# Marks, moved copies and banks at both ends of a two-block transformer kernel, and rotary tables spread by transfers

## The chip, the cores and the metric

The kernel runs on one core of a Trainium2 chip. The core has TensorE (PE, the matrix unit), VectorE (DVE), ScalarE (ACT) and GpSimd (POOL), which run their own instruction queues and wait for each other by semaphores, and SyncE (SP), whose queue issues all transfers of this kernel to the 16 DMA engines. The metric is the device time of one execution in microseconds.

## The reference

Two transformer blocks work one after the other on x of 32 sequences, 64 tokens each, 512 features, all in float32. The first block has 8 query heads and one head of keys and values, rotary positions that come from an input, and a gated MLP of width 2048; the second has 16 query heads in four groups, keys and values from a latent of 128, and no MLP. Both norms are scaled by a condition per sequence.

```python
def block0(x, pos_ids, t, ...):
    h = ada_rms(x, t, ln1_w, ln1_tw)          # x * rsqrt(mean(x*x)) * w * (1 + t @ tw.T)
    q, k, v = h @ Wq.T, h @ Wk.T, h @ Wv.T    # 8 heads, 1 head, 1 head of 64
    q, k = rope(q, pos_ids), rope(k, pos_ids) # x * cos(pos * freq) + rotated(x) * sin(pos * freq)
    x = x + softmax(q @ k.T / 8) @ v @ Wo.T
    h = ada_rms(x, t, ln2_w, ln2_tw)
    return x + silu(h @ Wg.T) * (h @ Wu.T) @ Wd.T

def block1(x, t, ...):
    scale, shift = split(t @ W_ada.T + b_ada)
    h = layernorm(x) * (1 + scale) + shift
    q, c = h @ Wq.T, h @ Wkd.T
    k, v = c @ Wku.T, c @ Wvu.T               # 4 groups of 32
    return x + softmax(rope(q) @ rope(k).T / sqrt(32)) @ v @ Wo.T
```

## The kernel before

**Tiling.** The 2048 tokens are cut into eight units of 256 tokens (four sequences). Features lie on the 128 partitions, so x of a unit is a tile of 128 x 4 x 256. Each unit passes through `attention0`, `mlp` and `attention1`. The MLP goes in eight steps of hidden blocks; each matrix product there is done with seven block products instead of eight, from sums of weight blocks (`combine` makes four sums per set of weights on VectorE or GpSimd during unit 0, `done_with` stores them to DRAM, and later units load them back). A set is a tile of 7 x 256 columns; five buffers with the tag `mw` hold sets, and `load_sets` issues the load of a set when a buffer comes free.

**Order of work.** The pieces of work are generators. Between the ends, `Order.run` picks the next piece by costs and latencies that the generators yield, so that attention of neighbouring units fills in between the MLP steps of the current one. A scheduler below that places each engine's instructions by their priority and its own timing, unless an order is forced. At both ends the order is written by hand: the string `FIRST` for the start and `LAST` for the end, one letter per piece: `a` and `b` are two units (0 and 1 at the start, 6 and 7 at the end), `m` a piece of the modulations, `i` a pair of idle matmuls (in `LAST`). TensorE is held to that order by `ordered`; the other engines are not.

**The start.** SP loads positions, constants, the first modulation weights, x and the attention weights. `first_angles` makes sine and cosine of position times frequency for units 0 and 1, a quarter of the partitions per sequence. `modulation` multiplies the condition with its weights, copies the product to SBUF (`rows`, L313), turns it on TensorE (`pt_mod`) and makes the scale s0a (later s0b, s1, t1). `rms` squares x on ScalarE and scales x by s0a, half on VectorE and half on GpSimd for the lean first two units (L518). `angles` makes the angles of two further units at a time; it is called at the end of `attention0` of units 1, 3 and 5, and its instructions may be placed earlier.

**Rotary tables.** The angles lie with 32 frequencies times 4 sequences on the partitions; the rotation of queries needs them with features on the partitions and sequences along the columns. `spread_out` (L409) does that with four matmuls by a matrix of zeros and ones, for sine and cosine together. `tables` calls it for units 2 to 7 and multiplies the PSUM result by the row of inverse roots into `cs` (L418, L419); units 0 and 1 use `tables_by_quarters`.

**PSUM.** Eight banks: two with the tag `at` for attention, two `gu`, four `acc`. In the middle attention uses `at` alone; at both ends `abank` goes around over all of them. `output` adds the output projection to x: at the end (`fine`) it works in four chunks of 128 features, two chunks in one bank (`po`, L535), each followed by an add on VectorE (L583) and a transfer out (L584). `context` of `attention1` copies its PSUM result to SBUF in two copies per bank on ScalarE (L911).

Of the kernel before, what the change touches and what calls it, by code (L numbers as in the profile page):

```python
# [1 line left out]

# [1 line left out]

# [6 lines left out]
F32 = mybir.dt.float32  # L11
# [6 lines left out]
P = 128  # L18
# [27 lines left out]
ROUND = 12582912.0  # L46
WARM = 11
STAY = 14103
FIRST = "aaaaaaa bb a mm aa bb a bbb aa b mm a bb aa a m b a b m b a b".replace(" ", "")
EARLY = 4  # L50

LAST = "aa b aa b iii b aa ii b bb bbb aa aa bb aa aaaa bbbb bb bbbb".replace(" ", "")
TWO_PI = float(np.nextafter(np.float32(2 * np.pi), np.float32(0)))


# [43 lines left out]
@contextmanager  # L99
def ordered(tc, engine):  # L100

    traced = tc.nc.cur_bb.bb.instructions
    start = len(traced)
    yield
    mine = [i for i in traced[start:] if i.engine == engine]
    info = mybir.DependencyInfo(mybir.DependencyClass.NoSync, mybir.DependencyReason.DATA)
    for one, other in zip(mine, mine[1:]):
        tc.add_manual_dep(other, one.name, info, reason="order")


@with_exitstack
def two_blocks(ctx: ExitStack, tc: tile.TileContext, a: dict, out: bass.AP):
# [69 lines left out]
    def load_positions(u0):  # L182
        t = work("pos", [P, 2 * S], f"pos_{u0}", 1).bitcast(I32)
        nc.sync.dma_start(t, a["pos"][:, u0 * S : (u0 + 2) * S])
        positions.append(t)

    load_positions(0)
    small = fixed([P, C_ALL])
    nc.sync.dma_start(small, a["small"])
# [56 lines left out]
    def load_sets(upto):  # L246
        for n in range(len(sets), min(upto, len(sequence))):
# [8 lines left out]
                nc.sync.dma_start(t[:, 0:4], kept[i])  # L256
            sets[n] = t

    def combine(n):

        if n < len(sequence) and sequence[n][1] < NP:
            t, a21 = sets[n], odd[n]
            e = nc.gpsimd if n < 2 else nc.vector
            e.tensor_tensor(t[:, 0], a21, t[:, 6], ALU.add)  # L264
            e.tensor_tensor(t[:, 1], t[:, 0], t[:, 4], ALU.subtract)
            e.tensor_tensor(t[:, 2], t[:, 4], a21, ALU.subtract)
            nc.gpsimd.tensor_tensor(t[:, 3], t[:, 5], t[:, 1], ALU.subtract)
# [26 lines left out]
    load_x(1)  # L294
    load_mod(1)
    nc.sync.dma_start(wo0, a["wo0"])


    def modulation(i):

        dst = (s0a, s0b, s1, t1)[i]
        ps = abank(f"ps_mod{i}")
        for k in range(KC):
            for c in range(KC):
                nc.tensor.matmul(
                    ps[c * B : (c + 1) * B, :P],
                    condT[:, k, :],
                    mods[i][c, k],
                    start=(k == 0),
                    stop=(k == KC - 1),  # L310
                )
        rows = work("latT1", [P, UT], f"rows_{i}", 1)[:, :P]
        nc.vector.tensor_copy(rows, ps[:, :P])  # L313
        yield 1.2, 0.5
        pt = abank(f"pt_mod{i}")
        nc.tensor.transpose(pt[:, :P], rows, ident)
        got = pt[:, :P].rearrange("p (c b) -> p c b", b=B)
        v = vecs[:, KC * i : KC * (i + 1)].unsqueeze(2).to_broadcast([P, KC, B])
        if i < 2:
            nc.vector.scalar_tensor_tensor(dst, got, 1.0, v, ALU.add, ALU.mult)  # L320
        elif i == 2:
            nc.vector.scalar_tensor_tensor(dst, got, 1.0, v, ALU.add, ALU.add)
        else:
            nc.vector.tensor_tensor(dst, got, v, ALU.add)
        yield 0.1, 0.0
# [3 lines left out]
    def angles(u0):  # L329
# [38 lines left out]
        nc.scalar.activation(acc, hi, AF.Sin, scale=TWO_PI)  # L368
        nc.scalar.activation(rnd, prod, AF.Sin, scale=TWO_PI)
        nc.vector.tensor_tensor(rnd, rnd, sign, ALU.mult)  # L370
        if u0 + 2 < NU:
            load_positions(u0 + 2)

# [32 lines left out]
    def spread_out(ps, of):  # L406

        for b in range(US):
            nc.tensor.matmul(ps[..., b, :], spread[:, b], of, start=True, stop=True)  # L409

    def tables(u, r):

        ps = abank(f"tab_{u}").rearrange("p (i b s) -> p i b s", i=2, s=S)
        spread_out(ps, angle[:, :, u * S : (u + 1) * S])
        cs = work("cs", [P, 2, UT], f"cs_{u}", 1)
        cos, sin = cs[:, 0], cs[:, 1]
        ps = ps.rearrange("p i b s -> p i (b s)")
        nc.vector.tensor_tensor(cos, ps[:, 0], r, ALU.mult)  # L418
        nc.vector.scalar_tensor_tensor(sin, ps[:, 1], sign_of, r, ALU.mult, ALU.mult)  # L419
        return cos, sin  # L420

    def tables_by_quarters(u, few, room):
# [82 lines left out]
    def rms(u, s, h, room, name):  # L505

        x = x_units[u]
        lean = "lean" in room
        sq = tile4(room, "h", f"sq_{name}") if lean else work("sq", [P, KC, UT], f"sq_{name}", 1)
        nc.scalar.activation(sq, x, AF.Square)  # L510
        if lean:
            parts = [sq[:, k] for k in range(KC)]
            c = KC // 2
            for e, part in ((nc.vector, slice(0, c)), (nc.gpsimd, slice(c, KC))):
                to = h[:, part].rearrange("p c (b s) -> p c b s", s=S)
                of = x[:, part].rearrange("p c (b s) -> p c b s", s=S)
                by = s[:, part, US * u : US * (u + 1)].unsqueeze(3).to_broadcast([P, c, US, S])
                e.tensor_tensor(to, of, by, ALU.mult)  # L518
# [55 lines left out]
    def output(u, cT, w, name, last=False, fine=False):  # L574

        x = x_units[u]
        for h in range(2):
            po = abank(f"po_{name}_{h}").rearrange("p (c t) -> p c t", c=2)
            for c in range(2):
                o = 2 * h + c  # L580
                project(po[:, c], w, slice(o * P, (o + 1) * P), cT)
                if fine:
                    nc.vector.tensor_tensor(x[:, o], x[:, o], po[:, c], ALU.add)  # L583
# [12 lines left out]
    def attention0(u, room, early=None, late=None):  # L596
# [28 lines left out]
        if lean:  # L625
            few = space(room, "few", 3 * S, f"quarters_{u}").rearrange("p (k c) -> p k c", c=S)
            root_by_quarters(r, eps0, few[:, 0], f"ms_a{u}")
            kv = keys_values()
            yield 1.7, 0.0
            turn = query(0)  # L630
# [3 lines left out]
            cos, sin, r = tables_by_quarters(u, few, room)  # L634
        else:
            cos, sin = tables(u, r)
        yield 1.0, 0.0

        qT = tile4(room, "qT", f"qT0_{u}")
        turn = turn or query(0)  # L640
# [117 lines left out]
    def attention1(u, room):  # L758
# [139 lines left out]
        def context(t, pTs):  # L898
# [9 lines left out]
                    )  # L908
            to = cT[:, :, t * P : (t + 1) * P].rearrange("p c (b s) -> p b c s", s=S)
            for b in range(2):  # L910
                nc.scalar.copy(to[:, b], cx[:, b])  # L911

        ps = []
        for t in range(2):
# [159 lines left out]
    load_mod(3)  # L1074

    first = work("p0", [P, 1024], "p0_0", 1)
    ahead = Job(attention0(1, {"ring": "1", "lean": True}, late=lambda: angles(2)), A0)
    streams = {
        "a": attention0(0, {"ring": "0", "lean": True, "p": [first[:, :512], first[:, 512:]]}, early),
        "b": ahead.pieces,  # L1080
# [1 line left out]
    }  # L1082
    with ordered(tc, mybir.EngineType.PE):
        for name in FIRST:
            next(streams[name], None)
# [168 lines left out]
```

## Time and profile before

| | |
|---|---|
| median of 3 runs | 1048.79 us (1048.55 to 1049.76) |
| profiled execution, its own time | 1047.82 us |
| its span, first to last instruction | 1046.0 us |
| TensorE clock granted, mean | 0.992 |
| busy: PE, DVE, ACT, POOL | 1007.5, 548.7, 334.1, 436.4 us |
| DMA | 198.53 MB, mean 190 GB/s |

Busy times are the union of an engine's instructions; a float32 matmul is recorded as two. The waits name the engine whose event came last before an instruction could start. In a timeline each row has the start, the time from first start to last end, the engine, the source line, the operation, output and inputs with their sizes and the count; in brackets the idle time of that engine just before, with what ended it. The page's slices cut the span in 40 equal parts of 26 us; the digits are tenths.

### The profile page before, as it was taken

How to read it: one execution, taken by the hardware profiler on the slowest of the kernel's cores; microseconds unless marked ns; L12 is line 12 of the kernel's file. 1: busy time of each engine (PE TensorE's matmuls, PEld its weight loads, DVE VectorE, ACT ScalarE, POOL GpSimd, SP SyncE). 2: the span in 40 equal slices, each digit the busy share in tenths (PEclk: the TensorE clock that was granted, in tenths of full speed). 3: DMA queues.
4: the chain of work that ended last, by engine and by line, in shares of the span. 5: the costliest groups of instructions: out<-in, count | busy, mean ns of one | idle time of the engine just before them, and what ended most of it. 6: DMA issues, size and time to landing. Idle time of an engine off the chain costs nothing.

```text
span 1046.0 us, 21558 instructions
## 1 busy us (share of the span) xinstructions
PE 1007.5 (96%) x8578; PEld 936.4 (90%) x8578; DVE 548.7 (52%) x1379; ACT 334.1 (32%) x683; POOL 436.4 (42%) x521
## 2 busy tenths in 40 slices
PE   7899999999999998999999999999999999999987
PEld 6679989998999998999999989899999899999875
DVE  4966656454355376444664366652465425543372
ACT  5333112244123242143340342242323512333141
POOL 3424545544244532445342354324553334642351
PEclk8989999999999999999999999999999999999999
DMA  8816886553655563673646646446745547565201
GB/s 279 314 60 202 275 299 244 195 175 144 230 198 185 171 213 125 233 247 104 229 163 231 233 141 212 160 155 219 259 165 193 180 167 250 185 235 202 79 1 40
DMA packets 68850, 198.53 MB, mean 190 GB/s; under 512 B 7312, under 2 KB 16272, under 8 KB 68368
## 3 DMA queue, kind: packets, MB, share of 16 engines
q1 hardware_dynamic: 68752, 197.17, 54.5%
q8 instruction: 68, 1.11, 0.4%
q14 instruction: 30, 0.25, 0.1%
HBM read 180.37 MB, written 16.78 MB: 188 GB/s over the span
## 4 chain that ended last, share of the span: by engine, by line
PE 81%; DVE 8%; POOL 4%; DMA 4%; issue 2%; ACT 1%; SPq 0%; ACTq 0%; DVEq 0%; POOLq 0%
PE gu L937 33%; PE down L996 16%; PE q L535 10%; PE po L535 10%; DMA set<-in_wmlp 3%; PE sc L875 2%; PE pp L570 1%; PE cx L902 1%; PE lat L535 1%; PE sc L689 1%; PE kv L535 1%; PE cx L710 1%; DVE set L264 1%; DVE sm L563 1%; DMA x<-in_x 1%
## 5 line engine op out<-in xcount | busy, mean ns | idle before, releaser
L937 PE MATMUL gu<-h,set 128*128 128x128 f32 x2048 | 288.6, 277 | 6.8 <-DVE c L956 6.3
L937 PEld LDWEIGHTS gu<-h,set 128*128 128x128 f32 x2048 | 259.4, 193 | 16.2 <-issue 11.3
L937 PE MATMUL gu<-hc,set 128*128 128x128 f32 x1536 | 215.7, 276 | 0.0
L937 PEld LDWEIGHTS gu<-hc,set 128*128 128x128 f32 x1536 | 193.9, 193 | 1.0 <-issue 0.6
L975 POOL TENSOR_TENSOR act<-c,c 128x384 f32<-128x384 f32 x64 | 66.4, 1037 | 212.1 <-DVE c L963 138.2
L996 PE MATMUL down<-td,set 128*128 128x128 f32 x1024 | 137.7, 276 | 3.7 <-POOL td L978 2.5
L996 PEld LDWEIGHTS down<-td,set 128*128 128x128 f32 x1024 | 125.5, 192 | 5.7 <-POOL td L978 3.5
L949 ACT COPY e<-gu 128x128 f32<-128x128 f32 x128 | 33.7, 264 | 260.9 <-PE gu L937 244.9
L535 PE MATMUL po<-cT,stays 128*128 128x256 f32 x480 | 109.4, 382 | 3.4 <-DVE x L583 1.8
L535 PE MATMUL q<-h,stays 128*128 128x256 f32 x480 | 109.4, 381 | 0.0
L996 PE MATMUL down<-act,set 128*128 128x128 f32 x768 | 109.4, 278 | 0.0
L963 DVE TENSOR_TENSOR c<-gu,u 128x256 f32<-128x256 f32 x128 | 53.4, 419 | 106.5 <-PE gu L937 106.2
L951 DVE TENSOR_TENSOR u<-e,gu 128x128 f32<-128x128 f32 x128 | 36.1, 282 | 129.7 <-ACT e L949 129.1
L535 PEld LDWEIGHTS po<-cT,stays 128*128 128x128 f32 x480 | 89.7, 192 | 15.9 <-DVE x L583 2.6
L996 PEld LDWEIGHTS down<-act,set 128*128 128x128 f32 x768 | 97.7, 192 | 5.3 <-issue 3.2
L535 PEld LDWEIGHTS q<-h,stays 128*128 128x128 f32 x480 | 90.1, 191 | 12.3 <-issue 0.4
L565 POOL TENSOR_TENSOR p<-p,sm 128x512 f32<-128x512 f32 x40 | 41.6, 1058 | 121.5 <-DVE sm L564 115.6
L546 POOL TENSOR_TENSOR qT<-u_q,v_q 128x512 f32<-128x512 f32 x30 | 38.1, 1270 | 89.0 <-DVE v_q L545 88.9
L1032 ACT ACT_TABLE_LOAD x35 | 44.9, 1283 | 55.6 <-DVE c L963 55.1
L589 DVE TENSOR_TENSOR x<-x,po 128x512 f32<-128x512 f32 x28 | 19.2, 687 | 72.9 <-PE po L535 72.9
L977 POOL TENSOR_TENSOR td<-act 128x256 f32<-128x256 f32 x64 | 46.7, 730 | 5.6 <-DVE act L974 0.9
L1032 ACT ACTIVATE c<-gu 128x128 f32<-128x128 f32 x64 | 17.7, 277 | 85.6 <-DVE c L963 77.7
(264 smaller groups left out, 1336.6 us busy)
## 6 DMA issues: line engine op xcount, KB each, us to landing
set<-sums SPq DMA_DIRECT2D x168, 512.0 KB, 5.7
set<-in_wmlp SPq DMA_DIRECT2D x192, 384.0 KB, 4.7
sums<-set SPq DMA_DIRECT2D x24, 512.0 KB, 4.8
x<-in_x SPq DMA_DIRECT2D x8, 512.0 KB, 5.6
mod<-in_mod SPq DMA_DIRECT2D x7, 512.0 KB, 5.4
a<-in_wmlp SPq DMA_DIRECT2D x24, 128.0 KB, 3.1
out_x<-x SPq DMA_DIRECT2D x12, 256.0 KB, 2.6
stays<-in_wo SPq DMA_DIRECT2D x2, 1024.0 KB, 8.0
```

Source lines behind the costliest of these rows:

```text
L535: nc.tensor.matmul(ps, w[:, k, cols], h[:, k, :], start=(k == 0), stop=(k == KC - 1))
L546: nc.gpsimd.tensor_tensor(dst, u, v, ALU.add)
L565: nc.gpsimd.tensor_tensor(p8, p8, sm.unsqueeze(2).to_broadcast(wide), ALU.mult)
L875: nc.tensor.matmul(sc[b * S : (b + 1) * S, j * P : (j + 1) * P], qT[of, j, cols], kb[of, 2 * t + b].rearrange("p g k -> p (g k)"), start=True,
L937: nc.tensor.matmul(ps, w[:, slot, k * P : (k + 1) * P], b[of][:, k], start=start and k == 0, stop=k == 1, skip_group_check=True)
L949: nc.scalar.copy(e, ps[:, 0])
L951: nc.vector.tensor_tensor(u2, e, ps[:, 1], ALU.add)
L963: nc.vector.tensor_tensor(c.rearrange("p (a b) t -> p a b t", b=2)[:, :, 1], ps[:, 2:4], u2.unsqueeze(1).to_broadcast([P, 2, HT]), ALU.add,)
L975: nc.gpsimd.tensor_tensor(act[:, 1:4], gate[:, 1:4], c[:, 1:4], ALU.mult)
L977: nc.gpsimd.tensor_tensor(td[:, 0:2], act[:, 1:3], act[:, 0:2], ALU.subtract)
L996: nc.tensor.matmul(sums_of[u][p][:, c], w[:, slot, c * P : (c + 1) * P], b[of], start=q % NP == 0 and i % 2 == 0 and c == 0, stop=q % NP = ...
L1032: nc.scalar.activation(gate[2][:, 0], gate[0][:, 0], AF.Silu)
```

## The change

1. *First loads.* The first loads on SP are held to the written order, from positions to the output weights: positions, constants, modulation weights, x of unit 0, both attention weights, x of unit 1, the next modulation weights.
2. *Marks.* `marks` takes the last VectorE instruction recorded at each `|` in `FIRST`. The sums of sets 2 to 4 (`sums_of_set`) are placed behind the first mark on VectorE, the angles of units 2 and 3 behind the second.
3. *Other engines.* `rows` of all four modulations is copied by ScalarE instead of VectorE. For unit 0 (`a0`) both halves of the scaled x are made by GpSimd. In `context` of the last unit (`slim`), one copy of each pair goes to VectorE.
4. *Idle matmuls.* Two in the first modulation, four after the root sums of unit 0, and three pairs (`i`) late in `FIRST`.
5. *End.* Each of the four chunks of `output` with `fine` gets a bank of its own, and in `LAST` the two contexts of unit 6 stand before the scores of unit 7.
6. *Tables.* `tables` of units 2 to 7 no longer uses `spread_out`. At the end of `angles`, `spread_table` writes the angles of the two units to DRAM (four transfers of 32 KB) and reads them back into a tile of 128 partitions (four transfers of 128 KB that read each row twice). `tables` multiplies from that tile. The yield after it is 0.0 where it was 1.0 for these units.

On SP's queue the eight transfers of the first pair stand at four places between the loads and stores of sets, the last two reads behind the load of the last set of unit 0; those of the other pairs stand together within a set or two. TensorE has 48 table matmuls less as recorded (24 in the program) and 12 idle matmuls more.

```diff
-FIRST = "aaaaaaa bb a mm aa bb a bbb aa b mm a bb aa a m b a b m b a b".replace(" ", "")
+FIRST = "aaaaaaa bb a mm aa bb a bbb | aa b mm a bb aa a m b a bi m b ii a b |".replace(" ", "")
-LAST = "aa b aa b iii b aa ii b bb bbb aa aa bb aa aaaa bbbb bb bbbb".replace(" ", "")
+LAST = "aa b aa b iii b aa ii b bb bbb aaaa aa bb aaaa bbbb bb bbbb".replace(" ", "")
...
+def latest(tc, engine):
+    return next(i for i in reversed(tc.nc.cur_bb.bb.instructions) if i.engine == engine)
+@contextmanager
+def after(tc, engine, mark):
+    traced = tc.nc.cur_bb.bb.instructions
+    start = len(traced)
+    yield
+    info = mybir.DependencyInfo(mybir.DependencyClass.NoSync, mybir.DependencyReason.DATA)
+    for one in [i for i in traced[start:] if i.engine == engine]:
+        tc.add_manual_dep(one, mark.name, info, reason="order")
...
+    first_loads = ExitStack()
+    first_loads.enter_context(ordered(tc, mybir.EngineType.SP))
     load_positions(0)
...
+    marks = []
     def combine(n):
+        with after(tc, mybir.EngineType.DVE, marks[0]) if 2 <= n < 5 else nullcontext():
+            sums_of_set(n)
...
     nc.sync.dma_start(wo0, a["wo0"])
+    first_loads.close()
...
-        nc.vector.tensor_copy(rows, ps[:, :P])
+        nc.scalar.copy(rows, ps[:, :P])
+        if i == 0:
+            idle(2)
...
         nc.vector.tensor_tensor(rnd, rnd, sign, ALU.mult)
+        spread_table(u0)
...
+    spread_tables = {}
+    def spread_table(u0):
+        rows = dram.tile([HALF0, 2, US, 2 * S], F32, tag=f"table{u0}", name=f"table{u0}")
+        for b in range(US):
+            nc.sync.dma_start(rows[:, :, b], angle[b * HALF0 : (b + 1) * HALF0, :, u0 * S : (u0 + 2) * S])
+        t = work("table", [P, 2, US, 2 * S], f"table_{u0}", 1)
+        for i in range(4):
+            of = rows[i % 2 * HALF1 : (i % 2 + 1) * HALF1].rearrange("f i b s -> f (i b s)")
+            to = t[i * HALF0 : (i + 1) * HALF0].rearrange("p i b s -> p (i b s)")
+            nc.sync.dma_start(to, of.unsqueeze(0).to_broadcast([2, HALF1, 8 * 2 * S]))
+        for u in range(2):
+            spread_tables[u0 + u] = t[..., u * S : (u + 1) * S]
     def tables(u, r):
-        ps = abank(f"tab_{u}").rearrange("p (i b s) -> p i b s", i=2, s=S)
-        spread_out(ps, angle[:, :, u * S : (u + 1) * S])
+        ps = spread_tables.pop(u)
...
-            for e, part in ((nc.vector, slice(0, c)), (nc.gpsimd, slice(c, KC))):
+            for e, part in ((nc.gpsimd if name == "a0" else nc.vector, slice(0, c)), (nc.gpsimd, slice(c, KC))):
...
                 o = 2 * h + c
+                if fine and c:
+                    po = abank(f"po_{name}_{h}_{c}").rearrange("p (c t) -> p c t", c=2)
...
             root_by_quarters(r, eps0, few[:, 0], f"ms_a{u}")
+            if u == 0:
+                idle(4)
...
-        yield 1.0, 0.0
+        yield 1.0 if lean else 0.0, 0.0
...
-                nc.scalar.copy(to[:, b], cx[:, b])
+                if slim and b:
+                    nc.vector.tensor_copy(to[:, b], cx[:, b])
+                else:
+                    nc.scalar.copy(to[:, b], cx[:, b])
...
-    ahead = Job(attention0(1, {"ring": "1", "lean": True}, late=lambda: angles(2)), A0)
+    def later_angles():
+        with after(tc, mybir.EngineType.DVE, marks[1]):
+            angles(2)
+    ahead = Job(attention0(1, {"ring": "1", "lean": True}, late=later_angles), A0)
```

More of the change, by code (lines that the diff above doesn't have):

```diff
@@ L1 @@
-from contextlib import ExitStack, contextmanager
+from contextlib import ExitStack, contextmanager, nullcontext
 import numpy as np
@@ L257, in load_sets, with sums_of_set @@
             sets[n] = t
+    marks = []
     def combine(n):
+        with after(tc, mybir.EngineType.DVE, marks[0]) if 2 <= n < 5 else nullcontext():
+            sums_of_set(n)
+    def sums_of_set(n):
         if n < len(sequence) and sequence[n][1] < NP:
@@ L409, in spread_out @@
             nc.tensor.matmul(ps[..., b, :], spread[:, b], of, start=True, stop=True)
+    spread_tables = {}
[10 more added lines that the diff above has]
+            spread_tables[u0 + u] = t[..., u * S : (u + 1) * S]
     def tables(u, r):
-        ps = abank(f"tab_{u}").rearrange("p (i b s) -> p i b s", i=2, s=S)
-        spread_out(ps, angle[:, :, u * S : (u + 1) * S])
+        ps = spread_tables.pop(u)
         cs = work("cs", [P, 2, UT], f"cs_{u}", 1)
         cos, sin = cs[:, 0], cs[:, 1]
-        ps = ps.rearrange("p i b s -> p i (b s)")
-        nc.vector.tensor_tensor(cos, ps[:, 0], r, ALU.mult)
-        nc.vector.scalar_tensor_tensor(sin, ps[:, 1], sign_of, r, ALU.mult, ALU.mult)
+        r, to = r.rearrange("p (b s) -> p b s", s=S), cs.rearrange("p i (b s) -> p i b s", s=S)
+        nc.vector.tensor_tensor(to[:, 0], ps[:, 0], r, ALU.mult)
+        nc.vector.scalar_tensor_tensor(to[:, 1], ps[:, 1], sign_of, r, ALU.mult, ALU.mult)
         return cos, sin
@@ L1084, in two_blocks @@
         for name in FIRST:
-            next(streams[name], None)
+            if name == "i":
+                idle(2)
+            elif name == "|":
+                marks.append(latest(tc, mybir.EngineType.DVE))
+            else:
+                next(streams[name], None)
     rest = [ahead]
```

## The prediction

> **What bounds the kernel now.** I read the page first (busy shares, slices), then the waits of TensorE by stage, then the timelines of the two ends.
>
> ```profile
> PE 1007.5 (96%) x8578; PEld 936.4 (90%) x8578; DVE 548.7 (52%) x1379; ACT 334.1 (32%) x683; POOL 436.4 (42%) x521
> PEclk8989999999999999999999999999999999999999
> ```
>
> TensorE is busy for 1007.5 of 1046.0 us; every other engine has half its time free. So what shortens the kernel is a matmul less, a TensorE gap less, or a matmul at full instead of half clock. The missing 38.5 us are not spread evenly: busy time by stage is 37.9 of the first 50 us, 20.6 of 50 to 73, 74.2 of 73 to 150, 820.1 of 150 to 980, and 54.6 of the last 66. The first 50 us lose 12.1, the long stage 9.9, the last one 11.4. The clock line is below 9 at the start only (8, 8 in the first and third slice of 26 us); by stage it is 0.80 between 50 and 73 us.
>
> Next, who TensorE waits for in the first 110 us and in the last 61 us (total, times, longest):
>
> ```profile
> PE pt_mod L316 <- DVE rows L313: 3.8, 2, 2.6
> PE kv L535 <- DVE h L518: 3.0, 1, 3.0
> PE row_b L409 <- DVE r_b L480: 1.8, 1, 1.8
> PE vt L670 <- DVE vT L653: 0.6, 1, 0.6
> ```
>
> ```profile
> PE po L535 <- DVE x L583: 2.8, 4, 1.3
> PE po L535 <- ACT cT L911: 1.6, 1, 1.6
> PE sc L875 <- POOL own_mw L546: 1.1, 1, 1.1
> PE po L535 <- ACT own_mw L911: 0.7, 1, 0.7
> ```
>
> These eight lines are 15.4 us, and the change touches all of them except the third. Last, the timeline of TensorE in the start and the row of the rotary tables:
>
> ```profile
> 14.76 3.78 PE L535 MATMUL kv<-h,stays 128*128 128x256 f32 x8 [2.98 <-DVE h L518]
> ...
> 28.17 1.99 PE L535 MATMUL kv<-h,stays 128*128 128x256 f32 x8
> ...
> 52.90 7.40 PE L535 MATMUL po<-cT,stays 128*128 128x256 f32 x32
> ...
> 68.56 2.07 PE L937 MATMUL gu<-h,set 128*128 128x128 f32 x8
> ...
> 77.78 1.50 PE L937 MATMUL gu<-h,set 128*128 128x128 f32 x12
> ```
>
> ```profile
> L409 PE MATMUL tab<-stays x48: 272/273/275, 165.7 to 772.0; 128*128 128x128 f32 x48
> ```
>
> The same eight matmuls of keys and values take 3.78 us after a gap and 1.99 us without one; eight of `gu` take 2.07 us at 68.56 and about 1.06 us later. The tables of units 2 to 7 are 48 matmuls in the full middle.
>
> **What the Trainium skill says.** (1) "TensorE: Matmul & The Clock Gate", Part 1 on the clock gate: the array runs at half clock after an idle window of about 3.4 us and at full clock after a busy one. The trace agrees: 3.78 against 1.99 us. (2) "PSUM — Partial Sum Buffer", bank collisions: TensorE and a reader have to be kept apart by bank, not by address. That is the `po` wait: in the last unit chunk 2 of a bank starts 0.51 us after chunk 1, behind a 0.42 us add. (3) "DMA: Bandwidth & Descriptors", Anatomy of one DMA: DMA engines wait for no semaphore, the issuing sequencer does, and a transfer has about 2 us of fixed cost. Here 128 KB land 3.1 us after issue. (4) "SBUF — State Buffer", Who interferes with whom: a VectorE operation with two SBUF inputs excludes a GpSimd operation. `set` L264 takes 0.41 us at least, 1.32 us at most.
>
> **The change part by part.** The start, in the order of TensorE:
>
> - *First norm.* Before, `rows` (L313) starts at 10.57 though its matmuls end at 9.09; it stands behind VectorE's angles. On ScalarE: 9.1 to 9.4, turn by 9.75, s0a (0.29) by 10.1. Then GpSimd scales both halves of h, 2 x 1.03 us (its two at 11.84 took 2.05), to 12.1. VectorE's half had ended at 14.71. The six added idle matmuls (0.27 each; 12 records of the final part's idles take 1.60 us) lie in the 1.70 us wait for `mod` and after the root sums, ending near 12.5. kv starts at 12.5 instead of 14.76: **2.2**. The reordered first loads leave `mod` and x_0 in the same places; `small` moves one place up, and x_1 (needed by 15) goes behind the second weight.
> - *Clock.* With a gap of under 1 us before kv instead of 2.98, kv takes about 2.0: **1.8**.
> - *6.8 us of sums moved.* Sets 2 to 4 put nine VectorE operations between 30.69 and 42.1 (0.41 us each alone, up to 1.32 against GpSimd), in a stretch, 30 to 50, where VectorE is 97% busy. They now stand behind the first mark, after the second rotation of unit 1; in that spot they take the place of eight angle operations. `rows` of the next two modulations goes to ScalarE. That removes the waits of 1.24, 0.29, 0.61 and 2.56, 4.7 in all; ScalarE's own row copy and the `cT` copies before `po` (1.5 us) put back about 1.0: **3.7**. `po` of unit 0 would start at 45.2 (52.90 before).
> - *The chain to the second norm* keeps its form (add 0.69, square 1.06, table load 1.28, root 0.31, reciprocal 0.55) and gets the fourth `rows` copy on ScalarE in front: **+0.3**. The 1.80 us wait stays, filled by the other six idles (1.6 us, inside gaps of 2.4).
> - *Clock again.* `gu` at 68.56 runs 2.07 + 1.92 + 1.06 where 1.06 + 1.06 + 0.61 is normal: **2.3**, if the idles hold the clock.
> - The 35 angle operations of units 2 and 3 all fall behind the second mark, eight more than before in the first MLP steps, 3.2 us of VectorE. Behind them wait `u`, `w`, `c`, and TensorE behind those through its two `gu` banks. I charge 0.7.
>
> Sum of the start 2.2 + 1.8 + 3.7 - 0.3 + 2.3 - 0.7 = **9.0**.
>
> The middle: the eight records of one table occupy 0.89 us (165.86 to 166.75 in the chain of waits), six times: **5.3**. On VectorE the two reads come from SBUF instead of PSUM, same size, 0.41 and 0.48; a GpSimd collision could add under 1 us each, hidden as VectorE has half its time free. The new cost is on SP's queue: 24 issues of 0.33 to 0.4 us, per pair of units four writes that wait for the angles and four reads that wait for the writes (128 KB; 3 us each step). Queued behind them are the weight sets. A set is 114/24 = 4.75 us of TensorE; five buffers mean that a load is issued 19 us before its use and lands in 5.7, so 13 us of slack hide it from unit 1 on. In unit 0 the sums are made two places ahead, slack 19 - 9.5 - 5.7 = about 4 us, and DMA is 0.87 busy; there the stop costs something, which the trace does not show: between 0 and 4 us, I take 1.0. Last reads for unit 2 stand behind a set load issued at 154.7, its use at 170.0: 11 us of cover. The scheduler lays all middle matmuls in another order, worth -2 to +2, taken as 0. Net **4.3**.
>
> The end: contexts of unit 6 go before the scores of unit 7. Scores then start at about 1015.4, when GpSimd's qT (1015.15) is there (wait of 1.10 gone), contexts' copies are done long before `po` (1.58 gone), and the `po` chunks have banks of their own (1.29 + 0.51 gone). `po` of unit 6 ends near 1024.3 instead of 1029.5. What is late next is the softmax of unit 7: its first banks are full 0.4 us later, VectorE gets two more adds (0.74) and loses a 0.43 wait, so GpSimd's last product ends at 26.6 instead of 25.98, and the last turn starts there. Its copy ends at 27.75, the last context at 28.7, before 33.37: **4.6**. VectorE and ScalarE halve the last copy, 0.2 (0 if they exclude each other on one bank, 0.37 at most). Four chunks then run 3 x 1.73 + 2.01 = 7.2 instead of 8.74: **1.5**. Sum 6.3, taken as **6.0**.
>
> Total 9.0 + 4.3 + 6.0 = 19.3. Span 1046.0 - 19.3 = 1026.7; its execution, 1047.82, becomes 1028.5; the median of the runs stands 0.97 above that execution: **1029.5**.
>
> **Rivals.**
> - *The start is given back.* Between 30 and 50 us DMA is 0.96 to 1.04 busy, so a front that comes 8 us earlier may meet its loads; the clock may drop all the same, and VectorE's moved sums may hold the softmax of unit 1. Against it: DMA idles from 55 to 79, so 24 us of slack lie behind it. Keeping 3 of 9: 1035.5.
> - *The middle is given back.* SP's stop in unit 0 costs its full 4 and the new order 2: 4.3 becomes -0.7: 1034.5. For it: VectorE waits 19.2 us in eight places for `set` in that stage. Against: TensorE waits only 3.1 from 110 to 170.
> - *Slower.* A table read that lands late stops VectorE in order at `cs`: behind it stand the `c` of the MLP, and TensorE after two gu banks. A landing L us after its planned place costs L - 15 (11 of cover, 4 of filled banks), three times; from L = 21.4 the 19.3 are gone, and at L = 24 the time is 1029.5 + 27 = 1056.5. Nothing in the profile speaks for transfers that take over 10 us.
> - *No effect*: ends and middle cancel, 1048.8.
>
> **How the numbers follow.** Chances: forecast 0.62, start given back 0.18, middle given back 0.12, slower 0.05, no effect 0.03. A measurement can tell 0.2%, about 2 us. Low end: start 10.5, middle 7.3, end 7 give 24.8, so 1024; high end: start 3, middle 0, end 6 give 9, so 1040. Beyond that lie the last two cases and a little of the first two, 0.15.
>
> **What would show it.** kv of unit 0 near 12.5 and 2 us long; `po` of unit 0 near 45; no half-clock `gu`; span slices at full clock from the second on; no `tab` row at 273 ns x48; no `po` waits for L583's successor; the last `po` chunk 7.2 us after the first. Wrong it would be if TensorE waits for `cs` or for `set` grow beyond 4 us, if kv stays at 3.78, or if the last turn waits for GpSimd more than 2 us.

## The result, and the profile after

The changed kernel takes 1050.24 us (median of 12 runs, 1045.90 to 1052.88) against 1049.34 us for the kernel before in the same comparison (12 runs): ratio 1.0008, 95% interval 0.9996 to 1.0021. Nothing was gained and nothing lost. The forecast was 1029.5 us with a range of 1024 to 1040, so it was 20.7 us too low and the time lies outside the range. The profiled execution of after took 1049.41 us, its span is 1047.6 us (before: 1047.82 and 1046.0).

The page of after, busy time and granted clock:

```profile
PE 1001.1 (96%) x8554; PEld 931.2 (89%) x8554; DVE 550.5 (53%) x1376; ACT 333.1 (32%) x684; POOL 436.9 (42%) x522
PEclk9999999999999999999999998999999999999999
```

TensorE is busy for 6.4 us less than before and still the span is 1.6 us longer: TensorE stands still for 8 us more. The clock line has lost its two 8s at the start, as forecast, and has one where before had none, in the 25th slice of 26 us, 629 to 655 us. The start, the end and the middle are taken one by one.

The start in the timeline of TensorE of after (columns: start, length, then the instruction group, and in brackets the idle time before it with what ended it):

```profile
12.03 1.89 PE L577 MATMUL kv<-h,stays 128*128 128x256 f32 x8
...
43.66 7.17 PE L577 MATMUL po<-cT,stays 128*128 128x256 f32 x32 [0.67 <-ACT cT L766]
...
59.87 1.16 PE L986 MATMUL gu<-h,set 128*128 128x128 f32 x8 [0.48 <-DVE h L573]
...
80.28 1.16 PE L1045 MATMUL down<-td,set 128*128 128x128 f32 x8 [2.16 <-DVE x L633]
```

The first `kv` starts at 12.03 (14.76 before) at full clock, `po` at 43.66 (52.90), the first `gu` at 59.87 (68.56), also at full clock. TensorE is 8.7 us ahead in this profile. One new gap follows at 80 us: 2.16 us for x.

The end of after, in the same view:

```profile
1033.84 0.66 PE L612 MATMUL pp<-stays,own_act 128*128 128x128 f32 x4 [1.09 <-POOL own_act L607]
...
1037.31 7.17 PE L577 MATMUL po<-own_mw,stays 128*128 128x256 f32 x32 [0.93 <-DVE own_mw L958]
```

The four waits of `po` for the adds to x are gone, and the last four output chunks run in one piece of 7.17 us. From the end of the last unit's MLP (ScalarE's first `ev`, 984.05 before and 991.06 after) to the end of the span it is 61.95 us before and 56.5 after: 5.4 us gained.

So in the traces both ends show about what was forecast, and the middle takes it all. These are the largest waits of TensorE between 110 and 987 us (total, times, longest), of before:

```profile
PE gu L937 <- DVE c L956: 6.3, 9, 1.8
PE pp L570 <- POOL p L565: 2.7, 2, 1.9
PE down L996 <- POOL td L978: 2.5, 5, 1.2
PE down L996 <- DVE set L265: 0.9, 2, 0.6
```

and the two largest of after:

```profile
PE down L1045 <- DMA set<-in_wmlp: 8.8, 3, 7.8
PE down L1045 <- POOL td L1027: 5.9, 3, 3.1
```

TensorE waited for the load of no weight set in that stage before; the last line is a wait for sums on one. No single wait was longer than 1.9 us. To see how the lead is lost, take the moment at which each unit's MLP ends, after against before, in us: unit 0 -4.1, unit 1 -7.3, unit 2 -7.3, unit 3 -4.5, unit 4 **+7.2**, then +7.6, +7.1 and +7.0. The order of work inside a unit changed, so one number is not exact (in the kernels below whose reads cost nothing, unit 4's mark is late by some 7 us, and the next mark takes that back), but the stretches between are: 2.8 us are lost between units 1 and 3, 12.1 us between units 3 and 5. In these stretches lie the transfers for the pairs 4/5 and 6/7. Here is the second, first SP's queue and then TensorE (its first line is the same twelve `down` matmuls shortly before):

```profile
631.94 3.48 SPq L444 DMA_DIRECT2D table<-stays  x4
636.81 1.94 SPq L449 DMA_DIRECT2D table<-table  x3
638.85 0.59 SPq L268 DMA_DIRECT2D set<-in_wmlp  x1
639.95 0.62 SPq L449 DMA_DIRECT2D table<-table  x1
```

```profile
631.75 1.50 PE L1045 MATMUL down<-td,set 128*128 128x128 f32 x12
...
652.14 1.19 PE L1045 MATMUL down<-act,set 128*128 128x128 f32 x4 [7.84 <-DMA set<-in_wmlp]
653.41 2.90 PE L1045 MATMUL down<-td,set 128*128 128x128 f32 x12
```

The chain of waits joins the two. The set whose load was issued at 638.85 landed 13.16 us later, and TensorE went on at once:

```profile
636.71 2.13 PE gu L986 x20
638.85 13.16 DMA set<-in_wmlp
653.41 2.90 PE down L1045 x12
```

The median of such a load over the whole execution is 4.9 us. After the gap twelve `down` matmuls take 2.90 us, where they took 1.50 at 631.75. Why the load took 13 us is seen in the stretch 651 to 658 us, where only the last of the four reads and what is left of the sets issued beside it are in flight; on the second line a stretch of ordinary middle (columns: us; busy us and counts of TensorE, its weight loads, VectorE, ScalarE, GpSimd; granted clock; mean busy share of the 16 DMA engines; GB/s):

```profile
651.00:658.00 7.00, 5.78 (x33) 5.54 (x34) 1.75 (x5) 0.37 (x1) 0.82 (x2) 0.62 0.13 51
300.00:340.00 40.00, 39.53 (x362) 37.60 (x361) 20.33 (x50) 12.95 (x30) 20.17 (x22) 1.00 0.61 209
```

0.13 of sixteen engines is two engines (0.125). Three of the four reads, 384 KB, stand ahead of the set in SP's queue; at 51 GB/s that is 7.7 us of work for these two engines, and a set that needs all sixteen would have to wait for them: it took 13.16 - 4.9 = 8.3 us more than usual.

The trace fits that. It records each update of the semaphores by which transfers report their landing; the load of a set has 16. Of those of the set issued at 638.85, fourteen come by 643.0, 4.2 us after the issue. The last two come at 651.5 and 652.0, right behind the last two updates of the third read, at 650.8 and 651.3. A read of the table has only three updates, one about 1 us after its issue and two at its end, where every other transfer of this kernel has 16. If an update stands for the part that one engine has moved, two of the sixteen parts of the set waited behind the reads, and fourteen were in time.

That SP issues no load for a while is no difference to before: between the last load ahead of the tables and the one at 638.85 lie 11 us, and at the same place of the kernel before (629.17 to 640.39) as many.

The code tells why it may be two: each read takes a block of 16 rows from DRAM and repeats it for 32 partitions, so the slowest dimension of its source is a 2. The Trainium skill states it outright in "DMA: Bandwidth & Descriptors", in the rules for kernel authors, row "Use all 16 engines": "an outermost dim of size c < 16 — e.g. a leading zero-stride broadcast of c copies — confines the whole DMA to at most c engines." The trace agrees: 0.13 of the engines at 51 GB/s. The prediction had drawn on that page for another sentence and passed over this one. What remained to be tested is whether the repeat costs the time of the kernel, against two other theories: SP's queue (24 issues that stand before weight sets and wait for the angles and writes) and the size of a transfer (128 KB).

### The profile page after: what moved, and what is told of

Read it like the earlier page. It is cut to its first block, busy times and chain, and to the rows that moved or that the text cites. A ratio compares the mean times of both kernels' runs of the same rounds, so it can differ in the third digit from the quotient of the medians.

```text
span 1047.6 us, 21404 instructions
## 1 busy us (share of the span) xinstructions
PE 1001.1 (96%) x8554; PEld 931.2 (89%) x8554; DVE 550.5 (53%) x1376; ACT 333.1 (32%) x684; POOL 436.9 (42%) x522
## 4 chain that ended last, share of the span: by engine, by line
PE 75%; DVE 9%; DMA 7%; POOL 4%; ACT 3%; issue 2%; SPq 1%; POOLq 0%; DVEq 0%; ACTq 0%
PE gu L986 30%; PE down L1045 15%; PE q L577 10%; PE po L577 9%; DMA set<-in_wmlp 5%; PE pp L612 2%; PE sc L921 2%; PE cx L948 2%; PE lat L577 1%; DMA table<-table 1%; PE kv L577 1%; DVE sm L605 1%; PE sc L735 1%; DVE mx L597 1%; DVE set L287 1%
## 5 line engine op out<-in xcount | busy, mean ns | idle before, releaser
L1045 PE MATMUL down<-td,set 128*128 128x128 f32 x1024 | 140.6, 280 | 10.8 <-POOL td L1027 7.1
L1045 PEld LDWEIGHTS down<-td,set 128*128 128x128 f32 x1024 | 127.7, 195 | 13.6 <-POOL td L1027 8.1
L1045 PEld LDWEIGHTS down<-act,set 128*128 128x128 f32 x768 | 97.8, 192 | 12.9 <-issue 10.2
```

Of the source, the lines that this page charges most:

```text
L1045: nc.tensor.matmul(sums_of[u][p][:, c], w[:, slot, c * P : (c + 1) * P], b[of], start=q % NP == 0 and i % 2 == 0 and c == 0, stop=q % NP = ...
```

## The experiments

Ratios are against the kernel before, run beside each, with 95% intervals. The median of before in the four groups was 1049.3, 1049.1, 1048.1 and 1048.3 us.

**Which part loses the time.** The change without its tables (`tables` with `spread_out` on TensorE and the planner's step at 1.0 as before; the edit is shortened):

```
@@ angles(u0)
-        spread_table(u0)
@@ tables(u, r)
-        ps = spread_tables.pop(u)
+        ps = abank(f"tab_{u}").rearrange("p (i b s) -> p i b s", i=2, s=S)
+        spread_out(ps, angle[:, :, u * S : (u + 1) * S])
@@ after the tables
-        yield 1.0 if lean else 0.0, 0.0
+        yield 1.0, 0.0
```

> The change without its tables: units 2 to 7 spread their tables on TensorE again, all else as in the changed kernel. Few engines (the reads that repeat each row run on few DMA engines, and the weight sets queue behind them there) and SP's queue (the eight more issues and their waits hold the sets up) both say that the two ends keep their 9 + 6 us and nothing is lost between: 1034 us (1031 to 1038). Front (the earlier front and VectorE's moved work cost the middle what the ends gain): 1045 to 1050.

Measured: 1036.92 us, ratio 0.9889 (0.9873 to 0.9906). The opposite, the kernel before with the three edits of the tables and nothing of the ends:

> The kernel before with the tables by transfers alone, both ends as before. Few engines and SP's queue: 5.3 us less matmul and some 20 us of waits for sets and tables, 1064 us (1056 to 1070). Front: 5 us faster than before, 1044.

Measured: 1068.53 us, ratio 1.0180 (1.0157 to 1.0203). The ends alone gain 12 us, the tables alone lose 19; together they would give 7 us lost, and the changed kernel has about 1, so the two are not quite additive, but the sign of each part is settled. It is the tables.

**Few engines, or the queue, or the size.** The same bytes without a repeat: each read is cut in two that read 16 different rows each. SP issues more, not less.

```
         for i in range(4):
             of = rows[i % 2 * HALF1 : (i % 2 + 1) * HALF1].rearrange("f i b s -> f (i b s)")
-            to = t[i * HALF0 : (i + 1) * HALF0].rearrange("p i b s -> p (i b s)")
-            nc.sync.dma_start(to, of.unsqueeze(0).to_broadcast([2, HALF1, 8 * 2 * S]))
+            for j in range(2):
+                at = i * HALF0 + j * HALF1
+                to = t[at : at + HALF1].rearrange("p i b s -> p (i b s)")
+                nc.sync.dma_start(to, of)
```

> The changed kernel with each of the four reads cut in two transfers of 16 rows, so that no transfer repeats rows: the same bytes, four more issues per pair. Few engines: the backlog goes, 1030 us (1027 to 1035), no wait of TensorE for a set over 2 us and none of VectorE for the tables. SP's queue: more issues, so 1050 to 1054. Front: 1050.

Measured: 1034.89 us, ratio 0.9867 (0.9846 to 0.9888). This is 15.4 us below the changed kernel, for one edit (14.8 by the two ratios). The DMA issues of this run (count, size of each, median us from issue to landing):

```profile
set<-sums SPq DMA_DIRECT2D x168, 512.0 KB, 5.7
set<-in_wmlp SPq DMA_DIRECT2D x192, 384.0 KB, 4.5
table<-table SPq DMA_DIRECT2D x24, 64.0 KB, 3.6
```

A read lands in 3.6 us, each has 16 updates of its semaphore, VectorE nowhere waits for a table and TensorE nowhere for the load of a set. With twice the issues in the queue, the theory of SP's queue, which expected 1050 us and more, falls.

The other direction, each read of the changed kernel issued twice:

```
-            nc.sync.dma_start(to, of.unsqueeze(0).to_broadcast([2, HALF1, 8 * 2 * S]))
+            for _ in range(2):
+                nc.sync.dma_start(to, of.unsqueeze(0).to_broadcast([2, HALF1, 8 * 2 * S]))
```

> The changed kernel with every one of its four reads issued twice. Few engines: the backlog doubles, another 10 us in front of the sets and tables of pairs 4 and 6, 1068 us (1060 to 1080). SP's queue: four more issues of 0.6 us per pair, mostly hidden, 1050 to 1054. Front: 1050.

Measured: 1073.41 us, ratio 1.0237 (1.0219 to 1.0255). TensorE's waits for the loads of sets grow from 8.8 to 23.0 us, and one wait for the tables is now the longest single wait of VectorE (in the changed kernel: 3.4, 1, 3.4):

```profile
DVE cs L460 <- DMA table<-table: 21.3, 3, 10.8
```

What both runs leave open is the size: the fast reads were also smaller. So I kept reads of 128 KB to 32 partitions and took away the repeat alone, by writing each block to DRAM twice:

```
-        rows = dram.tile([HALF0, 2, US, 2 * S], F32, ...)
+        rows = dram.tile([2, 2, HALF1, 2, US, 2 * S], F32, ...)
         for b in range(US):
-            nc.sync.dma_start(rows[:, :, b], angle[b * HALF0 : (b + 1) * HALF0, :, ...])
+            for k in range(2):
+                for j in range(2):
+                    at = b * HALF0 + j * HALF1
+                    nc.sync.dma_start(rows[j, k, :, :, b], angle[at : at + HALF1, :, ...])
...
-            nc.sync.dma_start(to, of.unsqueeze(0).to_broadcast([2, HALF1, 8 * 2 * S]))
+            nc.sync.dma_start(to, rows[i % 2].rearrange("k f i b s -> (k f) (i b s)"))
```

(The writes of a pair become sixteen of 16 KB; my expectation miscounts them as eight.)

> As after, but each 16-row block is written to DRAM twice, so that each of the four reads of a pair is still one transfer of 128 KB to 32 partitions, with 32 different rows instead of 16 rows read twice. Writes double (eight issues a pair, about 1.3 us more of SP), reads stay four. Theory of few engines (a source that repeats runs on two of sixteen engines): no repeat, so a read lands within 5 us and the time is that of the reads cut in two, 1035 us (1032 to 1039). Rival, the size of a transfer (128 KB to 32 partitions is slow, 64 KB is not): as after, 1048 to 1052, with reads that land 10 us and more after issue. Rival, the number of issues on SP: slower than after, 1052 or more.

Measured: 1039.79 us, ratio 0.9916 (0.9895 to 0.9937). The reads, as large as in the changed kernel, land in 5.5 us (median; 3.7 to 7.6). In the changed kernel the trace's updates have them land 6.3 to 15.9 us after issue, and the fourth read of the two later pairs after 12.1 and 15.9:

```profile
table<-table SPq DMA_DIRECT2D x12, 128.0 KB, 5.5
table<-stays SPq DMA_DIRECT2D x48, 16.0 KB, 1.9
```

Each of them has 16 updates again. So it is the repeat, not the size. The time is 1 us above the interval that I gave, and 4.9 above the reads cut in two; from the first `gu` to the end of unit 1 this profile loses 6.2 us on the kernel before, the one with the reads cut in two loses nothing (-3.6 and -3.9 us). From unit 1 on the two agree within 1 us. Here SP's queue seems to show, in unit 0. These lines of the run are from SP's timeline, from the chain of waits (a load of weights that the next steps need) and from TensorE's timeline, in this order:

```profile
84.69 4.47 SPq L447 DMA_DIRECT2D table<-stays  x7
89.28 0.97 SPq L268 DMA_DIRECT2D set<-in_wmlp  x2
```

```profile
112.62 7.52 DMA a<-in_wmlp
```

```profile
120.93 2.05 PE L989 MATMUL gu<-h,set 128*128 128x128 f32 x8 [4.54 <-DVE c L1008]
```

SP is held for 4.47 us by seven writes and again for 5.4 us in all by eight more between 100 and 111 us; the next loads leave later, one lands 7.52 us after its issue, VectorE's `c` comes behind it and TensorE waits 4.54 us, again followed by half clock (2.05 us for what takes 1.16). The version with four writes and eight reads has no such wait in unit 0. That the writes are what made this load late is read from the order of these lines; no run separates it from the reads and sets around it.

**Sets queued behind the reads in SP's queue, or on the engines?** The changed kernel with writes and repeating reads issued on ScalarE's queue (`nc.sync` to `nc.scalar` in both calls of `spread_table`):

> The changed kernel with the writes and the reads of the tables issued on ScalarE's queue; the reads still repeat their 16 rows. SP then issues no table transfer, so no weight set stands behind one in a queue. Theory of few engines: the sets still meet the reads on two of the sixteen engines, a set still takes over 10 us to land in units 2 and 4, and cs still waits: 1045 to 1056. Rival, the stop of SP's queue (its waits for the writes and the time of its issues): without it the time is that of the reads without repeats, 1032 to 1037.

Measured: 1059.48 us, ratio 1.0113 (1.0095 to 1.0130), 9 us above the changed kernel (11 by the two ratios). With no table transfer left on SP, the last of a group of repeating reads takes even longer, as the chain of waits has it twice:

```profile
411.12 18.38 DMA table<-table
...
654.63 19.94 DMA table<-table
```

```profile
DVE cs L459 <- DMA table<-table: 13.4, 2, 10.9
PE down L1045 <- DMA set<-sums: 1.8, 1, 1.8
PE down L1045 <- DMA set<-in_wmlp: 0.5, 2, 0.3
```

So the cost of the repeat does not come from SP's queue alone. The page of the skill that was cited above says it of the queues of SP and ScalarE, in its rules for kernel authors: to spread DMAs over them doesn't help the bandwidth, since all run on the same sixteen engines and interleave. The trace agrees: the loads now go out beside the reads rather than behind them, the reads (ended at 659.9, 664.6, 669.6 and 674.6 us the second time) and the late parts of the sets (660.2, 662.7, 664.8, 667.9 and 670.1) come by turns, and the last read takes 18.4 and 19.9 us instead of 12.1 and 15.9. What the queue does decide is who waits more. TensorE's waits for sets fall from 8.8 us to the 2.3 of the last two lines and the slowest load of a 384 KB set from 16.2 us to 10.4, while VectorE's waits for the tables rise from 3.4 to 13.4; TensorE's longest gap, 7.04 us before 432.88, now follows the late `cs` at 429.62. The same move for the reads without a repeat (the version at the end of this section, on ScalarE's queue):

> The version with non-repeating reads of 64 KB and the planner's step at 1.0, with writes and reads of the tables on ScalarE's queue. If SP's stop in unit 0 costs the 1.0 us that the prediction took (0 to 4), 1031 us; if ScalarE's waits for the writes hold its e and pT behind them, 1034 to 1038.

Measured: 1037.66 us, ratio 0.9901 (0.9885 to 0.9917), some 5 to 6 us worse than on SP; its trace has a new `q` wait of 3.6 us for ScalarE's `stays` (L894). The gain of 1 us that I had put on a free SP queue did not come; ScalarE's holding of the transfers may be what costs more. A like share of the 1059.48 us of the repeating reads may come from that, so that the two queues are best compared by what the repeat costs on each: 15.4 us on SP and 21.8 on ScalarE's queue (1059.48 against 1037.66; the planner's step differs too, which is taken up at the end of this section).

**The two ends apart.** The start alone (marks, idles, copies and norm, order of the first loads), and the end alone (`LAST`, banks of `fine`, half of the copies on VectorE):

> The start of the change alone (marks, idles, copies and norm on other engines, ordered first loads); tables and end as before. My prediction had 9.0 us for it, and the comparison of the traces shows TensorE 8.7 to 10.4 us ahead at its first gu operations: 1040 us if that is kept. The theory that the moved sums and angles then take some of it back in unit 0 (the wait of 2.2 us for x at 80 us, which both kernels with the new start have) gives 1041 to 1043. Above 1045 the start would be given back by more than any wait I have seen.

> The end of the change alone (order of the last turns, banks for the output chunks, half of the context copies on VectorE); start and tables as before. My prediction had 6.0 us, the traces show 5.4 from the end of the last MLP on: 1043 to 1044 us, with scores of the last unit waiting for POOL own_act about 1 us and po chunks back to back in 7.2 us. If the two ends do not add (start and end sums against 12.2 us for both), one of the two runs is above its value by 2 to 3 us.

Measured: 1042.10 us for the start, ratio 0.9946 (0.9928 to 0.9965), and 1043.92 for the end, 0.9956 (0.9940 to 0.9971). That is 6.0 and 4.2 us, each with an interval of some 2 us either way, 10.2 together where both in one kernel gained 12.2 (9.9 to 13.3 by its ratio). In the profile of the end alone, the end gains 5.3 us (end of the last MLP 0.3 later, span 5.0 shorter), as in the changed kernel. In that of the start alone, TensorE is 6.8 us ahead at the first `gu` and 3.5 at the end of unit 1; from there to the end of the last MLP nothing changes, and the end is 1.2 us longer than before (63.2 against 62.0), in the slowest of its eight runs. Some of the start is given back in unit 0, where its trace has the new wait too:

```profile
PE down L1025 <- DVE x L616: 2.1, 1, 2.1
```

To see whether the angles held behind the second mark cause it, I released them, in the version that follows (`angles(2)` without the mark):

> The version with non-repeating reads and the planner's step at 1.0, but the angles of units 2 and 3 no longer held behind the second mark. The wait of 2.2 us for x at 80 us goes if those operations are what makes x late; the prediction charged 0.7 for them. Gain 0.7 to 2: 1030.5 to 1031.7. If they come back into the stretch before the second norm, the first gu operations start up to 3 us later and the time is 1033 to 1035.

Measured: 1034.98 us, ratio 0.9879 (0.9860 to 0.9898); with the mark the same kernel takes 1031.7 to 1032.4, though the intervals still touch. The wait for x falls from 2.2 to 0.3 us, so the held angles are its cause. But now they stand before the second norm: the first `gu` starts at 66.81 instead of 60.66 (2.6 of it is there at the first `kv`, 15.42 against 12.81, behind later first loads), and at the top of TensorE's waits stands one that is 0.9 us long in the changed kernel:

```profile
PE qs_b L530 <- ACT sq_b L553: 3.6, 1, 3.6
```

So in the profiles the mark costs about 2 us at 80 us and saves some 3.5 before that; that it gains on the whole is likely by the medians and not shown.

**A version that is faster than both.** Reads cut in two, and the planner's step after the tables left at 1.0:

```
-        yield 1.0 if lean else 0.0, 0.0
+        yield 1.0, 0.0
```

> The kernel with reads cut in two (no repeats), with the step after the tables still counted as 1.0 us of TensorE by the planner, as before the change. Reads cut in two gained 2 us over the two ends alone, where 5.3 us of matmuls were taken out. Theory that the planner's order of the middle took 3 us back since the step counts as 0: 1032 us. Theory that the 3 us go elsewhere (VectorE's reads of the tables, waits in unit 0): as with the reads cut in two, 1034 to 1036.

> The version with non-repeating reads of 64 KB and the planner's step at 1.0, once more, for a narrower interval against before: 1032.4 us, ratio 0.985.

Measured, in two groups of runs of the same kernel: 1032.37 us, ratio 0.9853 (0.9834 to 0.9872), and 1031.74 us, ratio 0.9848 (0.9827 to 0.9870). It is 1.5% below the kernel before, and some 18 us below the changed one. Against the reads cut in two with the step at 0.0 (0.9867, 0.9846 to 0.9888) the intervals overlap: whether the planner's step brings 2.5 us is not shown. From the first `gu` to the end of the last MLP its first profile gains 3.4 us on the kernel before, where the ends without the tables lose 2.3 (-8.4 to -6.1 us): 5.7 us between the two (5.2 with its second profile), where the removed table matmuls were to bring 5.3. By the ratios of the runs the two versions are 3.8 to 4.3 us apart.

## Why the prediction was wrong

**Start, 9.0 us: right up to the first `gu`, not to the end of unit 0.** `kv` was forecast at 12.5 and 2.0 us long and came at 12.03 and 1.89; `po` at 45.2 and came at 43.66; full clock at `gu` was forecast and came. The first `gu` is 8.7 us earlier, where the terms before it sum to 7.4. Part of this nearness is luck: in the profiles of all kernels with the same start `kv` comes anywhere from 12.01 to 15.67. The term that was mis-sized is the last, "I charge 0.7" for the angles behind the second mark: that wait measures 2.1 to 2.2 us in every kernel with the new start and the mark, and is shown to be theirs by the kernel without the mark. By itself the start is worth 6.0 us (3.7 to 7.5). The profiles of kernels with the same start have the first `gu` anywhere from 59.87 to 65.00, with waits of 0.3 to 2.8 us for `mod` in front. Most of that spread is there at the first `kv`, where the load of x of unit 0 has landed 6.3 to 7.7 us after its issue; I had treated the times of the first loads as fixed.

**End, 6.0 us: right.** 5.4 us in the two traces, 4.2 us (3.0 to 6.3) by itself. The last chunks take 7.17 us (7.2 forecast), and the last turn waits for GpSimd 1.09 us, within the 2 us that I had named as the limit.

**Middle, 4.3 us: the step that failed.** By the medians the middle is about -13 us: the ends alone gained 12.2 us, the whole change lost 0.9. The saving in it is about right: 5.3 us forecast for the matmuls, 5.7 and 5.2 in the two profiles where the reads do not repeat and the planner's step is as before, some 4 by their runs. What failed is the cost of the new transfers: "128 KB; 3 us each step", taken from a transfer of the same size that does not repeat. I took the size as the price and did not look at the shape of the access. In its place the runs show reads that run on two engines, the last of four landing 12.1 us after its issue for the pair 4/5 and 15.9 for 6/7, and weight sets behind them that take 13 to 16 us instead of 4.9; without the repeat the same kernel takes 15.4 us less. The sign that the prediction had named came: TensorE's waits for `set` grew to 8.8 us, beyond its 4. (The prediction quotes about 2 us of fixed cost from the Trainium skill, "DMA: Bandwidth & Descriptors", Anatomy of one DMA; the page gives them there for transfers issued by GpSimd. Here SP issues all, and its writes of 32 KB land in 1.9 us, so that this did not mislead.) On this step rested three others:

- "13 us of slack hide it from unit 1 on" counted only SP's stop. A set that leaves late may use that slack, but one that also takes 13 us instead of 5 to land does not fit; its wait is 7.84 us, and about 1.4 us of half clock follow at the next twelve matmuls.
- "A landing L us after its planned place costs L - 15". The cover was worked out for the pair 2/3, whose last reads SP issued at 148 with their use at 163. For the pair 4/5 the read leaves closer to its use. In the changed kernel the read of 398.08 landed 12.12 us later and VectorE's `cs` waited 3.44 for it, so the cover is 8.7 us, and TensorE's wait of 3.06 for `td` at 420.51 follows. On ScalarE's queue the pair 4/5 gives 7.5 us (18.38 and a wait of 10.90), the pair 6/7 17.4 (19.94 and 2.54). One place was taken for all three.
- The rival *Slower* named the mechanism partly and the place wrongly: it saw the late table stop VectorE, not the late table reads delay weight sets on shared engines. "Nothing in the profile speaks for transfers that take over 10 us" was true of the profile before and was the reason for its chance of 0.05; the diff spoke for it, in the one word `to_broadcast`, and the row of the Trainium skill quoted above gives the rule. I looked for evidence in the trace of a kernel that had no such transfer.

**The stop of SP in unit 0, 1.0 us, between 0 and 4:** not contradicted. Between 62 and 180 us TensorE waits 2.4 us for sets in the changed kernel (1.4 and 1.0), 0.9 before, and the engines' share in that is not told apart. With the writes quadrupled some 6 us were lost in unit 0 in one profile, so the mechanism may be there, and what the change as made pays for it is open.

**The other rivals.** The start given back (3 of 9 kept, 1035.5 us) happened in part, 6.0 of 9. The middle given back was forecast as -0.7 instead of 4.3, against the -13 measured. The rival that names what came is *No effect*, "ends and middle cancel", with a chance of 0.03; it gave no mechanism, and that loss and gain came out equal is chance. Without repeats the changed kernel takes 1034.9 us, 5.4 above the forecast and inside its range, and with the planner's step left at 1.0 it takes 1031.7 to 1032.4, within 3 us: had the transfers been what the prediction took them for, its range would have held. The range was too narrow because it put only 2 in 10 on all the unknown costs of transfers that the profile could not show.

What stays open: how the loss divides between the sets, the tables and the re-laid order. Of the 15.4 us that the one edit of the reads restores, the waits for sets (8.8), for tables (3.4, on VectorE) and the longest of the `td` waits (3.06) with the half clock after the gap name most, but they overlap and some of the planner's order is in both.

## What to carry to other kernels

Before a transfer is priced by its bytes, look at the slowest dimension of its source: here a source that repeats rows through a leading dimension of 2 ran on two engines, and two parts in sixteen of the weight sets issued behind it waited for it. Cut such a transfer into pieces without a repeat; more issues of the right shape were cheaper here by 15 us than fewer of the wrong one. And where a change brings a kind of instruction that the trace of before doesn't have, the lack of a bad case in that trace is no evidence: its cover has to be worked out for each place that it is issued from, and its price bounded from its own access pattern.

## What the runs showed of the hardware that was not expected

- A DMA from DRAM whose source is 16 rows repeated twice (128 KB, four at a time) has three updates of its semaphore in the trace instead of 16. The last read and what was left of the sets beside it moved 51 GB/s on 0.13 of the DMA engines. Such a read lands 6.3 to 15.9 us after its issue, and the last of four after 18.4 and 19.9 us where they were issued on ScalarE's queue and the weight loads went out beside them. The same 128 KB as 32 different rows lands in 5.5 us, 64 KB as 16 rows in 2.2 to 3.6 us (medians).
- Such transfers hold up others on the engines that they use. Of a set of 384 KB issued behind three of them, fourteen of sixteen parts had landed after 4.2 us and the last two after 12.7 and 13.2 us; another took 16.2 us (median of the execution 4.9). With the reads on ScalarE's queue such sets were held up less, 10.4 us at most, and the reads more, and the kernel was 9 us slower.
- A gap of 7.84 us on TensorE costs more than itself: the next twelve matmuls take 2.90 us, where the same twelve took 1.50 before it.
